# A gated recurrence over rows: the next gates' products move into the branch, and x_par by rows is built from transposes

## The chip, the cores and the metric

The kernel runs on one core of a Trainium2 chip. The metric is the device time of one execution in microseconds (us); the time before is the median of three runs.

## The reference

Four graph layers work on x (16 graphs of 1024 nodes with 256 features, fp32) and a weighted adjacency adj (16 × 1024 × 1024, about 3% non-zero). Each layer normalizes x by rows, applies a ReLU, runs its graph operation and adds the result to x. Only layer 2 matters here. It is a recurrence over the nodes, one after the other:

```
for i in 0..1023:                        # for all 16 graphs
    x_par = row_i(norm_adjT) @ h         # parents' states, updated or not yet
    r, z  = sigmoid(split(x_i @ Wioux.T + x_par @ Wiouh.T + biases))
    hc    = tanh(x_i @ Wcoux.T + (x_par * r) @ Wcouh.T + biases)
    h_i   = z * x_par + (1 - z) * hc
```

A node needs the new states of only those earlier nodes that it has an edge with.

## The kernel before

Layers 0 and 1 run first, one graph at a time, then layer 2 for all graphs, then layer 3, one graph at a time. The change touches layer 2 alone.

Layer 2 walks over 8 blocks (t) of 128 nodes, each cut into 8 sub-blocks (s) of 16 nodes. A sub-block holds 16 nodes of 16 graphs, so 256 rows, kept as two groups g of 128. Inside a sub-block, nodes depend on each other only along short chains of edges. The kernel therefore doesn't go node by node. It repeats a *round* on all 256 rows, each time with the states of the round before, until no chain is longer. Three rounds are always run (K = 3). If the longest chain of a sub-block is longer, a branch runs `one_more`, and inside it a loop runs further rounds. The chain lengths come from the adjacency at the start of the layer (`levels`).

A round works on changes. `change` multiplies the change of the states, dh, by the sub-block's own adjacency `ai` and gets the change of x_par in columns (features on partitions), first in the PSUM tile `px` and then in SBUF as `dx`; it also adds it to `x`, the x_par in columns. `round_` then adds products of dx to three PSUM accumulators that live through the whole sub-block: `pr` for r, `pz` for z, `pc` for the candidate. Four products of 128×128 by 128×256 go to each. ACT and DVE take r, z and hc from them and make the new state. `pxr` is a fourth accumulator: x_par by rows (nodes on partitions), which the new state needs. `seed` starts the accumulators of a sub-block: pr, pz and pc are copied from the gates of the inputs, and pxr gets four transposes of x. Then each `change` adds two products `ai`·dh to pxr.

Other work of TensorE is placed between these steps. There are four kinds.

- *Base products* (`base_tasks`, pb, L360): for the next block, the parents' sum over all other blocks. For each of the 16 graphs 14 matmuls of 128×128 go into one PSUM tile pb, of which there is a single buffer, and DVE moves it to `bxt` (L363). The graph's inputs `ab` and `hb` (1.4 MB together) are loaded through SP's queue into two buffers each, and the load for the graph after the next waits until the present graph's buffer is free. In the first block one more input block is used, in the last block there are no base products.
- *Far products* (`far_tasks`, pf, L461): a finished sub-block's part in the later sub-blocks of its block; up to eight matmuls, moved to bxt by DVE (L464).
- *Near product* (pf, L633): its part in the very next sub-block; x of the next sub-block waits for it.
- *Gates of the next inputs* (`gate_tasks`): x_i times Wx for the next sub-block, two tasks for r (L439, evicted by ACT into `gr`, L441) and two for z and the candidate (L448, evicted by DVE into `gz`, L450). Near, far and gates share the two buffers of pf.

The order in the source: `fill()` is called three times in each of the three rounds, and each call runs some of the base tasks (spread over the block) and some of the queue `others` (far tasks and gates, spread over the sub-block). `one_more` has no fill. At the end of a block, `last_block` (L386) multiplies the states just stored by the last piece of the adjacency, graph by graph, after reading them back from DRAM.

The source order isn't the order on an engine: a scheduler reorders each engine's instructions when the program is built, within the stretches between branches. It doesn't move an instruction across a branch.

## Time and profile before

| what | value |
|---|---|
| median of three runs | 6301.03 us (6299.73 to 6306.5) |
| profiled execution, its own time | 6304.63 us |
| its span | 6302.8 us |
| mean granted TensorE clock | 0.93 |
| TensorE matmul busy | 5568.5 us (88%) |
| TensorE weight load busy | 3827.4 us (61%) |
| VectorE busy | 2503.2 us (40%) |
| ScalarE busy | 1412.6 us (22%) |
| GpSimd busy | 1043.2 us (17%) |
| first x of the recurrence to first product of layer 3 | 1780.6 to 4708.6 us |

The profiled execution is a single one, 3.6 us above the median. Busy shares are means over three stages with different limits; for the recurrence one reads windows of one block or one sub-block. An engine's idle time before an instruction is listed with what ended it: "<-DVE bxt L363" means that VectorE's instruction of line 363 on tile bxt released it, "<-PEq L619" that TensorE's sequencer came through the branch at line 619. In the timeline, x8 means eight records under one line; an fp32 matmul makes two records, an fp32 transpose one.

### The profile page before, as it was taken

The page shows a single profiled execution, that of the slowest core. Times are in us where ns is not written, and L with a number is a line of the kernel's source. Part 1 is how long each engine was busy: PE and PEld are TensorE (multiplying, and loading weights), DVE is VectorE, ACT ScalarE, POOL GpSimd, SP SyncE. Part 2 cuts the span into 40 slices and gives each one's busy share as a digit, 9 for nine tenths or more (in the row PEclk, how much of TensorE's full clock was granted, in tenths as well). Part 3 has the DMA queues.
Part 4 walks back from the last instruction along what each step waited for, and adds up shares of the span by engine and source line. Part 5 has one row for each costly group of instructions (what it writes and reads, how often), then busy time and mean ns, then how long its engine had stood idle before and what let it go on. Part 6 is the DMA issues. An engine that isn't in the chain of part 4 may idle for free. (4 is left out here: it accounts for less than half of the span.)

```text
span 6302.8 us, 63085 instructions
## 1 busy us (share of the span) xinstructions
PE 5568.5 (88%) x23167; PEld 3827.4 (61%) x23167; DVE 2503.2 (40%) x6257; ACT 1412.6 (22%) x3226; POOL 1043.2 (17%) x1429
## 2 busy tenths in 40 slices
PE   7888888888589898998989989898979999999998
PEld 3444444444378786876777778776755555555555
DVE  2333233332135454554554545454543333233332
ACT  1111111111012222222222212222222222222222
POOL 1222122221111111111111111111111111111110
PEclk9988999889799898998999989898989999999999
DMA  3222122220643332323223233321032212121110
GB/s 127 91 76 100 60 100 81 83 103 21 181 152 98 98 95 59 88 84 91 70 67 102 88 99 98 100 72 34 9 111 74 79 62 94 60 80 69 72 60 14
DMA packets 477355, 520.40 MB, mean 83 GB/s; under 512 B 30208, under 2 KB 428800, under 8 KB 474752
## 3 DMA queue, kind: packets, MB, share of 16 engines
q1 hardware_dynamic: 461056, 447.93, 22.0%
q0 software_dynamic: 15872, 67.18, 2.9%
q8 instruction: 219, 3.59, 0.2%
q14 instruction: 208, 1.70, 0.1%
HBM read 431.10 MB, written 83.95 MB: 82 GB/s over the span
## 5 line engine op out<-in xcount | busy, mean ns | idle before, releaser
L360 PE MATMUL pb<-ab,hb 128*128 128x128 f32 x3648 | 530.4, 286 | 59.7 <-DMA hb<-he_d 34.8
L360 PEld LDWEIGHTS pb<-ab,hb 128*128 128x128 f32 x3648 | 511.1, 201 | 101.5 <-issue 43.3
L152 PE MATMUL pa<-at,h 128*128 128x512 f32 x1024 | 478.2, 631 | 72.0 <-ACT h L142 72.0
L686 PE MATMUL pa<-at,h 128*128 128x512 f32 x1024 | 444.5, 595 | 31.4 <-ACT h L83 31.4
L719 PE MATMUL pa<-w,hT 128*128 128x256 f32 x2048 | 468.2, 384 | 0.0
L699 PE MATMUL ph<-w,ag 128*128 128x512 f32 x1024 | 452.7, 593 | 0.0
L152 PE MATMUL pa<-at,q 128*128 128x512 f32 x1024 | 443.7, 594 | 0.0
L157 DVE COPY ag<-pa 128x512 f32<-128x512 f32 x64 | 44.3, 692 | 980.1 <-PE pa L152 980.1
L719 PEld LDWEIGHTS pa<-w,hT 128*128 128x128 f32 x2048 | 385.7, 193 | 46.5
L152 PEld LDWEIGHTS pa<-at,h 128*128 128x128 f32 x1024 | 206.2, 203 | 337.1 <-issue 241.9
L686 PEld LDWEIGHTS pa<-at,h 128*128 128x128 f32 x1024 | 195.8, 191 | 270.9 <-issue 267.6
L520 DVE TENSOR_TENSOR r<-r,x 128x256 f32<-128x256 f32 x450 | 173.3, 427 | 451.4 <-ACT r L519 451.4
L152 PEld LDWEIGHTS pa<-at,q 128*128 128x128 f32 x1024 | 193.6, 190 | 250.3 <-issue 237.7
L519 ACT ACTIVATE r<-pr 128x256 f32<-128x256 f32 x450 | 148.7, 382 | 844.4 <-PE pr L479 844.4
L699 PEld LDWEIGHTS ph<-w,ag 128*128 128x128 f32 x1024 | 191.1, 190 | 214.8 <-issue 214.0
L479 PE MATMUL pc<-wh,drx 128*128 128x256 f32 x1288 | 310.8, 384 | 10.4 <-DVE drx L522 10.4
L479 PE MATMUL pr<-dx,wh 128*128 128x256 f32 x1288 | 314.5, 383 | 0.0
L479 PE MATMUL pz<-wh,dx 128*128 128x256 f32 x1288 | 310.7, 380 | 0.0
L541 DVE TENSOR_TENSOR w<-w,hc 128x256 f32<-128x256 f32 x450 | 188.4, 454 | 266.8 <-ACT hc L540 266.8
L479 PEld LDWEIGHTS pc<-wh,drx 128*128 128x128 f32 x1288 | 237.4, 190 | 79.1 <-DVE drx L522 29.4
L704 ACT ACTIVATE junk<-hh 128x512 f32<-128x512 f32 x256 | 161.2, 630 | 527.3 <-DVE hh L702 527.3
L479 PEld LDWEIGHTS pr<-dx,wh 128*128 128x128 f32 x1288 | 242.2, 193 | 42.7 <-issue 3.3
(168 smaller groups left out, 8478.1 us busy)
## 6 DMA issues: line engine op xcount, KB each, us to landing
at<-in_adjT SPq DMA_DIRECT2D x128, 1024.0 KB
ab<-in_adj SPq DMA_DIRECT2D x128, 512.0 KB
x<-in_x SPq DMA_DIRECT2D x16, 1024.0 KB
x_d<-x POOLq DMA_DIRECT2D x16, 1024.0 KB, 7.5
he_d<-h POOLq DMA_DIRECT2D x16, 1024.0 KB, 5.1
heT_d<-hT POOLq DMA_DIRECT2D x16, 1024.0 KB, 4.5
he<-heT_d SPq DMA_DIRECT2D x16, 1024.0 KB
hb<-he_d SPq DMA_DIRECT2D x16, 1024.0 KB
```

Of the source, the lines that this page charges most:

```text
L152: nc.tensor.matmul(pa, h[:, mt, c * P : (c + 1) * P], at[:, mt, n0 : n0 + 512], start=mt == 0, stop=mt == NT - 1)
L157: nc.vector.tensor_copy(ag[:, c, n0 : n0 + 512], pa)
L360: nc.tensor.matmul(pb[:, c], hb[:, j, c * P : (c + 1) * P], ab[:, j], start=j == jts[0], stop=j == jts[-1])
L479: nc.tensor.matmul(to, lhsT, rhs, start=False, stop=True, skip_group_check=True)
L519: nc.scalar.activation(r[:, e], pr[:, e], AF.Sigmoid)
L520: nc.vector.tensor_mul(r[:, e], r[:, e], x[:, e])
L541: nc.vector.tensor_mul(w[:, g], w[:, g], hc[:, g])
L686: nc.tensor.matmul(pa, h[:, mt, c * P : (c + 1) * P], at[:, mt, n0 : n0 + NH], start=mt == 0, stop=mt == NT - 1)
L699: nc.tensor.matmul(ph, ag[:, c, (t0 + t) * P : (t0 + t + 1) * P], w1[:, c, e * 512 : (e + 1) * 512], start=c == 0, stop=c == DC - 1)
L704: nc.scalar.activation(junk, to, AF.Square, accum_out=sq[:, t, e : e + 1])
L719: nc.tensor.matmul(po, hT[:, k, t * P : (t + 1) * P], w2[:, k], start=k == 0, stop=k == HC - 1)
```

## The change

There are two edits.

1. x_par by rows. `seed` no longer transposes x into pxr, and `change` no longer adds the two products `ai`·dh. In their place `round_` calls `to_rows` after the products into pr: four transposes of dx (of x in the first round), which are accumulated in pxr.
2. Gates. The four gate tasks of the next sub-block no longer go to the queue that `fill` empties. If the branch for further rounds is taken, `one_more` runs them: two before its round and two in its fills. If it isn't taken, an else arm runs all four. Their list is turned round, since `one_more` takes from its end.

```diff
-                return (gr, gz), deque([task_r(0), task_r(1), task_z(0), task_z(1)])
+                return (gr, gz), [task_z(0), task_z(1), task_r(0), task_r(1)]
...
-            def seed(base, gr, gz):
+            def seed(gr, gz):
                 nc.scalar.activation(pr, gr, AF.Copy)
-                for g in range(G2):
-                    for c in range(DC):
-                        nc.tensor.matmul(pxr[:, g, c * P : (c + 1) * P], base[:, c, g * GR : (g + 1) * GR], ident,
-                                         is_transpose=True, start=g == 0 and c == 0, stop=True, skip_group_check=True)
...
             def change(dh, x, ai):
...
-                for g in range(G2):
-                    add(pxr[:, g], aig[g], dh[:, g])
...
+            def to_rows(dx, first):
+                for g in range(G2):
+                    for c in range(DC):
+                        nc.tensor.matmul(pxr[:, g, c * P : (c + 1) * P], dx[:, c, g * GR : (g + 1) * GR], ident,
+                                         is_transpose=True, start=first and g == 0 and c == 0, stop=True,
+                                         skip_group_check=True)
...
             def round_(...):
                 for e in range(DC):
                     for c in range(DC):
                         add(pr[:, e], wh[:, c, e * P : (e + 1) * P], dx[:, c])
+                to_rows(dx, first)
...
-            def one_more(x, rx, h, ho, ai):
+            def one_more(x, rx, h, ho, ai, tasks=()):
+                tasks = list(tasks)
+                def fill():
+                    if tasks:
+                        tasks.pop()()
...
                 dx = change(dh, x, ai)
-                r = round_(dx, x, rx, None, lambda: None, h)
+                fill()
+                fill()
+                r = round_(dx, x, rx, None, fill, h)
...
                     if s + 1 < NS:
                         sub = load_sub(t, s + 1, dp)
                         gx, tasks = gate_tasks(he, s + 1)
-                        others.extend(tasks)
...
-                    with tc.If(n_more[0][s] > 0, preferred_fallthrough_block=False):
-                        one_more(x, rx, h, ho, ai)
+                    with tc.If(n_more[0][s] > 0, preferred_fallthrough_block=False) as more_or_not:
+                        one_more(x, rx, h, ho, ai, tasks)
...
+                    if tasks:
+                        with more_or_not.Else():
+                            for task in tasks:
+                                task()
```

## The prediction

> **What bounds the kernel now.** I read first the busy shares, then the windows of one block of the recurrence (block 4, where no extra round runs), then the groups of instructions with shapes kept apart (window 1780 to 4680), then the timeline. The two stages around the recurrence are untouched by the diff, so only the 2.93 ms from 1781 to 4709 us count.

> Windows of block 4, one per sub-block (columns: width, then busy us and count of PE, PEld, DVE, ACT, POOL, then TensorE clock, DMA share, GB/s):

> ```profile
> 3366.80:3406.60 39.80, 38.66 (x205) 30.89 (x204) 22.39 (x50) 10.13 (x24) 7.05 (x11) 1.00 0.33 105
> 3520.10:3552.90 32.80, 32.23 (x178) 27.09 (x177) 18.00 (x48) 10.13 (x24) 4.51 (x9) 1.00 0.41 122
> ...
> sum 323.00, PE 301.81 PEld 251.51 DVE 159.30 ACT 80.88 POOL 54.73; mean PE 37.73 PEld 31.44 DVE 19.91 ACT 10.11 POOL 6.84
> ```

> TensorE is busy 38.66 of 39.80 us while VectorE has 22.39: TensorE's own work sets the length. Of the block's 21.2 us of TensorE idleness some 12.6 lie in the hand-over to the next block, so the rounds hold about 8.6. They have so little because other products (pb, far, gates) stand in each round's waits. Groups of instructions, then the timeline of the very last sub-block, which has no such filling:

> ```profile
> L360 PE MATMUL pb<-ab,hb 128*128 128x128 f32 x3137 | 458.2, 282 | 8.4 <-DMA hb<-he_d 3.3 <-DVE bxt L387 3.1 <-DVE bxt L363 1.4
> L448 PE MATMUL pf<-wx,hs 128*128 128x512 f32 x496 | 236.3, 595 | 3.4 <-PEq L621 2.0 <-PEq L619 1.4
> L439 PE MATMUL pf<-hs,wx 128*128 128x256 f32 x496 | 126.9, 381 | 0.0
> L479 PE MATMUL pxr<-dh,ai 128*128 128x256 f32 x388 | 104.2, 390 | 0.0
> L633 PE MATMUL pf<-bd,h 128*128 128x128 f32 x448 | 72.6, 311 | 83.5 <-DVEq L621 57.3 <-PEq L619 12.5 <-DVE h L542 7.2
> ```

> ```profile
> 4660.82 1.13 PE L497 MATMUL px<-ai,ho 128*128 128x128 f32 x8 [1.75 <-DVE ho L542]
> 4661.78 1.03 PE L479 MATMUL pxr<-ho,ai 128*128 128x256 f32 x4
> 4662.65 1.89 PE L479 MATMUL pr<-dx,wh 128*128 128x256 f32 x8
> 4664.38 1.89 PE L479 MATMUL pz<-wh,dx 128*128 128x256 f32 x8
> 4666.14 1.99 PE L479 MATMUL pc<-wh,drx 128*128 128x256 f32 x8
> 4669.89 1.13 PE L497 MATMUL px<-ai,dh 128*128 128x128 f32 x8 [1.75 <-DVE dh L542]
> ```

> An fp32 matmul is two records, a transpose one. From starts: px 0.9 us, the pxr adds 0.86, pr, pz, pc 1.73 each; then 1.9 us from pc's end until tanh and the DVE adds let the next px go. Between px's end and pr lie 0.94 us for copying dx, which the pxr adds fill exactly. So a bare round has two holes, **1.92** and **0.94** us.

> [...] pb has one buffer, and where products into it follow each other (last_block) the trace shows the bubble:

> ```profile
> 3305.57 1.22 PE L386 MATMUL pb<-ao,hr 128*128 128x128 f32 x4 [0.51 <-DVE bxt L387]
> ...
> 1745.57 3.81 PE L360 MATMUL pb<-ab,hb 128*128 128x128 f32 x32 [3.34 <-DMA hb<-he_d]
> 1750.55 3.81 PE L360 MATMUL pb<-ab,hb 128*128 128x128 f32 x32 [1.18 <-DMA hb<-he_d]
> ```

> [...] here the 1.4 MB of a batch (ab and hb), issued from 3001.40, moved between 3002.4 and 3007.2:

> ```profile
> 3002.40:3007.20 4.80, 4.77 (x30) 4.35 (x30) 2.69 (x7) 0.38 (x1) 0.29 (x1) 1.00 0.91 296
> ```

> so 5.7 to 6 us from release to data[...]. [...] the block hand-over runs at 0.78, the bare rounds with 1.9 us gaps at 1.00. [...]

> **The change part by part**, with the instruction order of both built programs, which matters more than the diff, since a scheduler places instructions between branches.

> *x_par by rows.* Removed: two pxr adds (0.86 us) in each later round. Added: four transposes of dx between pr and pz; before, those in the first round ran at 0.44 us for four (four records, next start 0.44 to 0.49 later). First round: moved only. Per block 16 × (0.44 − 0.86) = −6.7 us of TensorE work. But the adds sat in the 0.94 hole, and the transposes are on the path (pr, transposes, pz, pc back to back; drx is ready 3.5 us after pr begins, TensorE reaches pc after 3.9). So it pays only where something else fills the hole.

> *Gates.* Eight matmuls per sub-block: 4 at 0.43 and 4 at 0.86 (L439, L448 starts), 5.16 us, with two 0.47 us ACT evictions and two 0.69 us DVE ones. They leave the queue that fill() empties and go to the branch. In the else arm they hide the 1.92 us until h and the wait of near (L633); their evictions hide under near and the x add (1.7 us; gr 0.67 plus the pr copy 0.60 is less). No DMA moves; POOL's hs copy is done earlier.

> *What the scheduler makes of it.* In blocks 0 to 6 the built program issues, right after the branch of sub-blocks 0 to 3 and **ahead of near**, a burst of 24 to 31 pb matmuls; then few pb in the rounds, and none at all from the fourth or fifth sub-block's end on. Before, none stood there: 41, 31, 36, 36, 26, 18, 18, 18 were spread over the rounds. Near is queued behind the burst, and behind near x, pr and the whole round. The burst's work (0.223 us each: the opening phase runs 16 of them from 1675.36 to 1678.93) is not new, but it is now where nothing needs cover, and two things are new.

> (a) Bubbles in the burst. It crosses two batch ends (14 matmuls each): 2 × 0.55 us for pb's one buffer. And the load of batch b+2 may start only when b's buffer is free: 6.0 us later data, while b+1 occupies 3.1 + 1.1, so 1.8 us more. 2.9 us × 4 per block = +11.6. Bounds: 1.1 us each if loads keep up; some 4 if they take the 7 us per batch of the opening phase (from 1738 to 1746).

> (b) Cover gone. Holes left open, walked through the new order: sub-block 0: 0.58+0.27+0.36+0.72=1.9; 1 to 3: 1.3, 1.0, 1.0; 4: 2.3; 5: 5.0; 6: 5.5; 7: 0.8+2×(1.92+0.94)=6.5. Sum 24.5 against 8.6: +16. Bounds: 0.5 to 1.3 times that, since far evictions on DVE may shift the holes.

> Per block −6.7+11.6+16=+21, times 7: **+147**. Block 7 has no pb before or after; it loses the gates as filling: −6.7 against about +15 of holes, **+8**.

> *Taken branch.* 29 of 64 sub-blocks take it (from the inputs' adjacency), 33 extra rounds. Before, an extra round costs near's wait (57.3/22 = 2.6 us) and 1.1 for px beside 6.9 of matmuls. Now gates fill these, and in 13 sub-blocks the burst covers near's wait: −3 × 13; in the other 16, where near still waits for h: −1 each. **−55** (bounds −20 and −80).

> Sum: 147+8−55 = +100 on the profiled execution's 6304.6; its time lies 3.6 above the median of 6301.0, so the median should be **6401**.

> **The rivals.** *Faster:* the gates turn waits into work and TensorE stays full. Then only −6.7×8 and −55 and the else arms' share of near's wait (12.5) remain: 6301−54−55−12 = **6180**. For it: 83.5 us idle before near. Against it: the burst, and bare rounds at the end of each block. It decides below an added idleness of 15 us per block (I count 28). 8%. *Worse:* the loads also slip to 7 us and each burst's stall brings a half-clock window (3.4 us wide in the clock record, half lost): 28 × (1.1+1.7) more, **6480**; for it the 0.78 at hand-overs, against it the 1.00 over 1.9 us gaps. 20%. *Bubbles hidden:* loads keep up and half of (b) holds: −50−57, **6295**, no change; 4%. *Not what it says:* the transposes overwrite instead of adding; then values differ, and the time is that of the forecast. The forecast itself: 68%.

> **Numbers.** A measurement of this kernel can tell 0.2%, 12.6 us. Slower takes the forecast and the worse case, 0.88; same 0.04; faster 0.08. The range, 6325 to 6510, runs from the forecast with bubbles at their low bound and most cover kept to the worse case with (b) at its high bound.

> **What would show it.** After: pb (L360) with idleness before it of some 80 us, by DVE bxt and DMA hb; near's idleness fallen from 83.5 below 40; sub-blocks 0 to 3 of a block longer by 4 to 10 us (gates and pb of others moved in), 5 and 6 hardly shorter though they lost 4 us of pb; PE's busy sum lower by some 60 us while the stage is longer. Wrong if pb's idleness stays under 20 us, or if sub-blocks 5 and 6 fall by over 3 us.

## The result, and the profile after

The changed kernel takes **6492.8 us** (median, 6491.0 to 6500.55) against 6300.4 us before on the same chip: 1.0306 times the time before, 95% interval 1.0288 to 1.0324. The forecast was 6401 with a range from 6325 to 6510. So the sign is right and the time lies in the range, but the loss is 192 us where 100 was worked out.

The profiled execution has a span of 6490.9 us and a mean clock of 0.922. On the page's busy line TensorE is busier than before (5588.9 us against 5568.5), although its products should take some 60 us less:

```profile
PE 5588.9 (86%) x23167; PEld 3824.9 (59%) x23167; DVE 2468.4 (38%) x6257; ACT 1408.7 (22%) x3226; POOL 1019.6 (16%) x1429
```

Windows of block 4 after, one per sub-block (columns as before). Shown are sub-blocks 0, 1 and 5, and the sum:

```profile
3430.90:3479.40 48.50, 45.48 (x265) 39.32 (x266) 17.37 (x43) 10.04 (x24) 4.21 (x8) 0.94 0.52 134
3479.40:3523.10 43.70, 41.39 (x231) 33.80 (x230) 21.10 (x49) 10.05 (x24) 7.66 (x14) 1.00 0.38 121
...
3645.90:3679.40 33.50, 29.74 (x142) 23.78 (x140) 17.68 (x45) 9.98 (x25) 4.44 (x9) 0.95 0.26 76
...
sum 348.40, PE 306.21 PEld 251.69 DVE 155.67 ACT 80.36 POOL 51.82; mean PE 38.28 PEld 31.46 DVE 19.46 ACT 10.04 POOL 6.48
```

Sub-block 1 went from 39.8 to 43.7 us. Sub-block 5 has 36 fewer matmul records (142 against 178) and is no shorter: 33.5 against 32.8. The block's sum rose by 25.4 us. Groups of instructions in the recurrence (window 1780 to 4880, shapes apart):

```profile
L360 PE MATMUL pb<-ab,hb 128*128 128x128 f32 x3200 | 435.4, 287 | 97.3 <-DMA hb<-hn_d 36.1 <-DMA hb<-he_d 27.3 <-DVE bxt L363 18.9
L479 PE MATMUL pr<-dx,wh 128*128 128x256 f32 x1288 | 351.9, 416 | 34.6 <-DVE dx L496 32.9 <-DVE bxt L464 1.7
...
L386 PE MATMUL pb<-ao,hr 128*128 128x128 f32 x448 | 136.4, 460 | 113.9 <-DMA hr<-hn_d 59.2 <-DVE bxt L387 46.6 <-issue 6.7
...
L493 PE MATMUL px<-ai,dh 128*128 128x128 f32 x776 | 118.7, 299 | 128.6 <-DVE dh L545 65.9 <-DVE dh L557 62.6
...
L647 PE MATMUL pf<-bd,h 128*128 128x128 f32 x448 | 65.5, 294 | 17.1 <-DVE h L545 7.8 <-DVEq L631 6.2 <-POOL ai L416 3.1
```

The idle time ahead of the base products went from 8.4 to 97.3 us, two thirds of it ended by a load. Near's fell from 83.5 to 17.1. The holes of the rounds opened: ahead of px for dh 128.6, ahead of pr for dx 34.6. Ahead of last_block's products (L386) 113.9 us stand in place of 96.8. The same three groups before:

```profile
L479 PE MATMUL pr<-dx,wh 128*128 128x256 f32 x1288 | 314.5, 383 | 0.0
...
L386 PE MATMUL pb<-ao,hr 128*128 128x128 f32 x448 | 136.4, 460 | 96.8 <-DVE bxt L387 46.6 <-DMA hr<-hn_d 42.4 <-issue 7.3
...
L497 PE MATMUL px<-ai,dh 128*128 128x128 f32 x776 | 112.4, 287 | 51.7 <-DVE dh L548 36.8 <-DVE dh L542 14.7
```

The timeline at the end of block 4's sub-block 0 shows the burst; gates of the else arm, then base products, and only then near:

```profile
3463.68 3.60 PE L448 MATMUL pf<-wx,hs 128*128 128x512 f32 x8
3467.12 2.08 PE L439 MATMUL pf<-hs,wx 128*128 128x256 f32 x8
3469.04 0.38 PE L360 MATMUL pb<-ab,hb 128*128 128x128 f32 x2
3469.93 3.39 PE L360 MATMUL pb<-ab,hb 128*128 128x128 f32 x28 [0.52 <-DVE bxt L363]
3474.88 3.52 PE L360 MATMUL pb<-ab,hb 128*128 128x128 f32 x28 [1.55 <-DMA hb<-hn_d]
3478.24 1.06 PE L647 MATMUL pf<-bd,h 128*128 128x128 f32 x8
```

**Three shares of the recurrence.** To compare kernels I split its length (first x to first product of layer 3) into TensorE's idle time (neither matmul nor weight load), the clock loss (half of the time that TensorE was busy while the clock was granted at half) and the rest, which stands for the work at full clock. All three are worked out from the trace, in us. The clock loss is an estimate: it assumes that work at half clock lasts twice as long (in before, six records into pr took 2.65 us at half clock and 1.46 at full). A row's shares are those of one profiled execution, which lies up to 12 us from the median.

| kernel | median | ratio to before (95%) | recurrence | idle | clock loss | rest |
|---|---|---|---|---|---|---|
| before | 6300.4 | 1 | 2928.0 | 306.7 | 127.8 | 2493.5 |
| after | 6492.8 | 1.0306 (1.0288 to 1.0324) | 3105.6 | 457.1 | 178.9 | 2469.5 |
| e1 rows only | 6288.8 | 0.9989 (0.9980 to 0.9997) | 2912.4 | 319.0 | 156.7 | 2436.7 |
| e2 gates only | 6513.6 | 1.0354 (1.0340 to 1.0368) | 3118.2 | 445.9 | 137.5 | 2534.8 |
| e3 hold base | 6320.4 | 1.0040 (1.0026 to 1.0053) | 2937.7 | 344.8 | 145.1 | 2447.8 |
| e4 before branch | 6228.6 | 0.9892 (0.9877 to 0.9908) | 2854.8 | 284.8 | 107.7 | 2462.3 |
| e5 three buffers | 6417.8 | 1.0201 (1.0187 to 1.0215) | 3058.3 | 426.9 | 154.9 | 2476.4 |
| e6 one in arms | 6303.5 | 1.0014 (1.0007 to 1.0021) | 2923.4 | 329.0 | 139.3 | 2455.1 |
| e7 straight, old rows | 6217.6 | 0.9882 (0.9867 to 0.9897) | 2836.8 | 248.6 | 67.3 | 2520.9 |
| e8 hand-over only | 6261.8 | 0.9944 (0.9932 to 0.9957) | 2873.4 | 279.7 | 93.2 | 2500.5 |
| e9 hold, hand-over | 6302.9 | 1.0009 (1.0000 to 1.0018) | 2924.7 | 329.9 | 145.8 | 2449.0 |
| e10 best, two tiles | 6167.4 | 0.9792 (0.9778 to 0.9805) | 2786.2 | 239.6 | 42.6 | 2504.0 |
| e11 before, two tiles | 6232.8 | 0.9897 (0.9882 to 0.9912) | 2856.4 | 307.5 | 72.6 | 2476.2 |
| e12 after, two tiles | 6393.8 | 1.0156 (1.0141 to 1.0171) | 3010.3 | 429.2 | 123.7 | 2457.3 |

Each ratio is to the kernel before on the same chip in the same series; its medians there were 6295.6 to 6300.4. From before to after: idle +150, clock loss +51, rest −24, and 10 us that lie ahead of the recurrence. That is the 188 us between the two profiled spans.

### The profile page after: what moved, and what is told of

Same layout as the page of the kernel before. It is cut to its first block, busy times and chain, and to the rows that moved or that the text cites. A ratio compares the mean times of both kernels' runs of the same rounds, so it can differ in the third digit from the quotient of the medians.

```text
span 6490.9 us, 63160 instructions
## 1 busy us (share of the span) xinstructions
PE 5588.9 (86%) x23167; PEld 3824.9 (59%) x23167; DVE 2468.4 (38%) x6257; ACT 1408.7 (22%) x3226; POOL 1019.6 (16%) x1429
## 5 line engine op out<-in xcount | busy, mean ns | idle before, releaser
L360 PE MATMUL pb<-ab,hb 128*128 128x128 f32 x3648 | 501.1, 290 | 156.7 <-DMA hb<-he_d 67.1
L360 PEld LDWEIGHTS pb<-ab,hb 128*128 128x128 f32 x3648 | 477.0, 204 | 195.2 <-issue 110.6
L479 PE MATMUL pr<-dx,wh 128*128 128x256 f32 x1288 | 351.9, 416 | 34.6 <-DVE dx L496 32.9
L479 PE MATMUL pz<-wh,dx 128*128 128x256 f32 x1288 | 311.2, 380 | 0.0
L479 PEld LDWEIGHTS pr<-dx,wh 128*128 128x128 f32 x1288 | 255.0, 208 | 92.8 <-issue 47.3
L479 PE MATMUL pc<-wh,drx 128*128 128x256 f32 x1288 | 305.4, 380 | 0.6
L479 PEld LDWEIGHTS pc<-wh,drx 128*128 128x128 f32 x1288 | 242.6, 190 | 49.4 <-issue 13.9
L728 PE MATMUL pt<-ident,hh 128*128 128x128 f32 x1024 | 193.1, 325 | 83.3 <-DVE hh L724 74.2
```

The source lines that it names most:

```text
L360: nc.tensor.matmul(pb[:, c], hb[:, j, c * P : (c + 1) * P], ab[:, j], start=j == jts[0], stop=j == jts[-1])
L479: nc.tensor.matmul(to, lhsT, rhs, start=False, stop=True, skip_group_check=True)
L728: nc.tensor.transpose(pt[:, t * P : (t + 1) * P], hh[:, t, k * P : (k + 1) * P], ident)
```

## The experiments

Where nothing else is said, a diff is against the changed kernel; it is cut to its core.

**e1: the first edit alone.** The gates go into the queue that fill() empties, as in the kernel before.

```diff
-                return (gr, gz), [task_z(0), task_z(1), task_r(0), task_r(1)]
+                return (gr, gz), deque([task_r(0), task_r(1), task_z(0), task_z(1)])
...
+                        others.extend(tasks)
...
-                        one_more(x, rx, h, ho, ai, tasks)
+                        one_more(x, rx, h, ho, ai)
```

> The first edit alone: x_par by rows from transposes of the change, gates as before in the fill queue. The built program has no burst of base products ahead of near. Theory (the gates' place lets the scheduler put the burst ahead of near and leaves the rounds bare): this run is faster than before, some 6250 us (-161 x 0.42 us of TensorE work, +15 us in the 33 bare extra rounds), base products' idleness stays under 20 us. Rival (the transposes on the path are the cause): slower, 6370 us or more (161 x 0.44 us on the path).

Measured: 0.9989 of before. The rest fell by 57 us (by count, 54 without the extra rounds and 68 with them), but idle rose by 12 and clock loss by 29. In block 7, which has no base products to fill a hole, the edit costs 13 us: idle +6, clock loss +15, rest −8. In its groups the hole that the pxr products used to cover shows as a wait for dx, and near waits as before:

```profile
L479 PE MATMUL pr<-dx,wh 128*128 128x256 f32 x1288 | 336.0, 401 | 24.8 <-DVE dx L496 24.8
...
L636 PE MATMUL pf<-bd,h 128*128 128x128 f32 x448 | 76.5, 323 | 84.6 <-DVEq L624 57.0 <-PEq L622 12.3 <-DVEq L622 8.1
```

So the first edit is not what slows the kernel, and it is worth hardly anything by itself.

**e2: the second edit alone.** Gates in the arms, x_par by rows as before: transposes of x in seed and two pxr products in each change.

```diff
+                for g in range(G2):
+                    add(pxr[:, g], aig[g], dh[:, g])
...
-                to_rows(dx, first)
```

> The second edit alone: gates in both arms of the branch, x_par by rows as before (transposes of x at the start, adds of the adjacency's products in each change). The built program has bursts of 28 to 30 base products ahead of near. Theory: slow like the changed kernel, 6480 to 6560 us, idleness before base products near 90 us. Rival (transposes are the cause): 6300 to 6420 us.

Measured: 1.0354, as the theory expected. The whole loss comes with the gates in the arms. It is 0.0048 more than with both edits, so beside gates in the arms the first edit saves some 30 us. By shares, gates in the arms bring idle +139, clock loss +10 and rest +41; the first edit on top of them (after against e2) brings +11, +41 and −65.

**e3: both edits, but no burst.** The base tasks that fill() issues are ordered behind the last near product, so none can stand ahead of it.

```diff
-                        for _ in range(-(-len(todo) // left)):
-                            todo.popleft()()
+                        with ExitStack() as held:
+                            if todo is base_todo and last_near is not None:
+                                held.enter_context(tc.issue_after(last_near.ins))
+                            for _ in range(-(-len(todo) // left)):
+                                todo.popleft()()
```

> Both edits, and the base products that fill() issues in a sub-block may not be issued before the near product of that sub-block (an ordering on TensorE, no wait). The built program has no burst, and the base products stand in the rounds as before. Theory: the loss is gone and the first edit's gain shows, 6210 to 6280 us; near's idleness below 30 us. Rival (the gates standing in a row at the branch, in arms of their own, cost the time): stays above 6400 us.

Measured: 1.0040, which neither side expected: 168 us less than after (from the ratios), yet 23 us over before in the same series, where the theory had it faster. Its groups show what stays:

```profile
L360 PE MATMUL pb<-ab,hb 128*128 128x128 f32 x3136 | 454.5, 279 | 18.7 <-DVE bxt L363 7.7 <-issue 3.8 <-DVE bxt L387 3.1
...
L493 PE MATMUL px<-ai,dh 128*128 128x128 f32 x776 | 127.0, 309 | 115.1 <-DVE dh L557 70.0 <-DVE dh L545 42.0
...
L651 PE MATMUL pf<-bd,h 128*128 128x128 f32 x448 | 62.0, 282 | 32.3 <-DVEq L635 20.7 <-DVE h L545 7.6 <-POOL ai L416 2.1
```

The burst's 97.3 us are down to 18.7, but px still waits 115.1 us. So that wait doesn't come from the burst; e4 shows that it goes with the gates' place in the arms.

**e4: both edits, the gates in straight code just ahead of the branch, none in the arms.**

```diff
-                    with tc.If(n_more[0][s] > 0, preferred_fallthrough_block=False) as more_or_not:
-                        one_more(x, rx, h, ho, ai, tasks)
+                    for task in tasks:
+                        task()
+                    with tc.If(n_more[0][s] > 0, preferred_fallthrough_block=False):
+                        one_more(x, rx, h, ho, ai)
```

> Both edits, but the four gate tasks stand ahead of the branch in straight code, and neither arm has any. The built program has no burst (one base product ahead of near). Theory: it is the else arm that makes the scheduler place the burst, so this is fast too, 6220 to 6290 us. If gates as filling in the taken arm are worth what the prediction said (55 us), it is some 40 us slower than the run with held base products; if they are worth little, within 15 us of it. Rival (gates out of the fill queue leave the rounds bare, whatever the scheduler does): above 6400 us.

Measured: 0.9892, as expected, faster than both kernels. It is 92 us faster than e3, where the expectation had it slower or alike. Its groups:

```profile
L360 PE MATMUL pb<-ab,hb 128*128 128x128 f32 x3139 | 460.0, 279 | 5.7 <-DVE bxt L387 3.1 <-DVE bxt L363 2.2 <-issue 0.5
...
L493 PE MATMUL px<-ai,dh 128*128 128x128 f32 x776 | 117.5, 293 | 64.2 <-DVE dh L557 41.3 <-DVE dh L545 19.5
L386 PE MATMUL pb<-ao,hr 128*128 128x128 f32 x448 | 113.8, 398 | 82.7 <-DVE bxt L387 39.5 <-DMA hr<-hn_d 30.4 <-POOL ao L382 8.1
...
L645 PE MATMUL pf<-bd,h 128*128 128x128 f32 x448 | 61.7, 282 | 15.4 <-DVEq L633 11.9 <-DVEq L631 3.4
```

Near waits as little as after (15.4), px nearly as little as before (64.2), there is no burst, and the hand-over (L386) waits less than in either. The built order says how, and the trace agrees: gates that the source has ahead of the branch run partly behind it, where near or last_block would wait. This corrects a sentence in the section on the kernel: the scheduler does place instructions on the other side of a branch. In no run here did it take them out of an arm.

**e5: the changed kernel with a third buffer for ab and hb,** the load two graphs ahead, and one buffer each for gr, gz and hs.

```diff
-                    ab = big.tile([P, NT, P], F32, name="ab")
+                    ab = big.tile([P, NT, P], F32, name="ab", bufs=3)
...
-                    hb = big.tile([P, NT, D], F32, name="hb")
+                    hb = big.tile([P, NT, D], F32, name="hb", bufs=3)
...
-                            if b + 1 < B:
-                                load(b + 1)
+                                load(1)
+                            if b + 2 < B:
+                                load(b + 2)
```

> The changed kernel whole, with three buffers each for the inputs ab and hb of the base products instead of two, and the load issued two graphs ahead; gr, gz and hs get one buffer each to make room. The burst of base products after the branch stays (32 to 35 of them). Theory (part of the burst's cost is the wait for a load that may start only when a buffer is free): the idle time of pb that ends with a DMA, 63 us in the recurrence of the changed kernel, goes, and with it some of the half-clock windows; 6400 to 6460 us. Rival (the burst costs because of where it stands and by pb's single PSUM buffer, and a load that comes earlier only lets TensorE reach the next wait earlier): 6480 to 6510 us, with pb's idle time put down to DVE bxt instead.

Measured: 1.0201, within the theory's range. In its timeline three crossings of a graph's end in a burst cost 0.52 us each and no load is waited for; one of them:

```profile
3419.82 0.94 PE L361 MATMUL pb<-ab,hb 128*128 128x128 f32 x6 [0.52 <-DVE bxt L364]
```

Of the gain, 47 us lie in the recurrence (idle −30, clock loss −24, rest +7) and 29 ahead of it, where the opening phase of base products is paced by the same loads (first x at 1762 in place of 1791).

**e6: one gate task of four in the arms,** three ahead of the branch.

```diff
+                    while len(tasks) > 1:
+                        tasks.pop()()
                     with tc.If(n_more[0][s] > 0, preferred_fallthrough_block=False) as more_or_not:
```

> Both edits, but only one of the four gate tasks (half of z and the candidate, two of the eight products) in each arm; the other three stand ahead of the branch. In the built order the burst after the branch is still there in sub-blocks 0 to 4, with 14 to 20 base products instead of 24 to 31. Theory (the loss comes from the burst that the else arm brings and grows with it; the gates in the arms cost their share besides): about half of the burst's 170 us and a quarter of the arms' 92 us on top of 6229, so 6310 to 6370 us. Rival 1 (an else arm costs its whole price whatever stands in it): over 6440 us. Rival 2 (only the number of gates in the arms counts): 6240 to 6260 us.

Measured: 6303.5 us, just under the theory's range and outside both rivals'. With half the burst the base products' idle time is still 86.5 us, ended mostly by pb's eviction, with loads no longer among the first three:

```profile
L360 PE MATMUL pb<-ab,hb 128*128 128x128 f32 x3168 | 443.9, 288 | 86.5 <-DVE bxt L363 49.2 <-issue 11.3 <-ACT pc L485 6.9
```

So the loss grows with what stands in the arms: none, one task, four tasks give 0.9892, 1.0014, 1.0306. The idle time ahead of pb does not grow with it: it is nearly that of after (97.3), in a kernel 184 us faster. What parts the two kernels lies elsewhere, ahead of px (73.7 in place of 157.9 us), of last_block (84.7 in place of 113.9) and of pr for dx (13.7 in place of 34.6). The bubbles in the burst are thus not what parts the two; the cover that the rounds and the hand-over lose, to the burst and to the arms, weighs more.

**e7: e4 without the first edit** (diff against e4).

```diff
+                for g in range(G2):
+                    add(pxr[:, g], aig[g], dh[:, g])
...
-                to_rows(dx, first)
```

> The gates in straight code ahead of the branch, none in the arms, and x_par by rows as in the kernel before (transposes of x in seed, two pxr products in each change), so the faster version without the first edit. Theory (with gates and base products left to fill the holes, the first edit is worth its arithmetic, 6.7 us per block): 6265 to 6290 us. Rival (as by itself in the kernel before, it is worth about a tenth of a per cent, and moving the gates to just ahead of the branch brought the whole gain): 6228 to 6248 us.

Measured: 0.9882 (0.9867 to 0.9897), which can't be told from e4's 0.9892, and lies below both ranges: without the first edit the kernel is not slower. The rest is 59 us larger than in e4, but idle is 36 and clock loss 40 us smaller. In its groups pr doesn't wait (25.6 us in e4), pc waits 15.2 for drx instead, and the hand-over less:

```profile
L479 PE MATMUL pc<-wh,drx 128*128 128x256 f32 x1288 | 313.5, 385 | 15.2 <-DVE drx L522 15.2
...
L386 PE MATMUL pb<-ao,hr 128*128 128x128 f32 x448 | 106.3, 377 | 61.1 <-DVE bxt L387 35.9 <-DMA hr<-hn_d 15.5 <-POOL ao L382 6.4
```

The products that the first edit saves were work in a hole; with them there, the clock loss is smaller (67.3 us against e4's 107.7).

**e8: the kernel before, with the gates of the block's last sub-block alone ahead of the branch** (diff against before).

```diff
                         gx, tasks = gate_tasks(he_next, 0)
-                        others.extend(tasks)
+                        ahead = list(tasks)
...
+                    for task in ahead:
+                        task()
                     with tc.If(n_more[0][s] > 0, preferred_fallthrough_block=False):
```

> The kernel before, with only the gate tasks that a block's last sub-block makes for the next block taken out of the queue and put in straight code just ahead of the branch; all other gates stay in the queue, and x_par by rows is as before. In the built order ten of those sixteen records now stand after the branch and between the first products of last_block. Theory (the gain of the straight versions lies at the seven hand-overs, whose last sub-blocks took 55 us less in all than before, because the gates fill the wait for the states' reload and keep TensorE's clock): 6235 to 6260 us. Rival (the gain lies in the waits of near inside the blocks, and the hand-over only shows work moved there): 6280 to 6305 us.

Measured: 0.9944, 6261.8 us: 2 us above the theory's range, 18 below the rival's. The last sub-blocks of blocks 0 to 6 took 473.6 us in place of 514.9. By the medians that is about half of the gain of e7. In e7 the same sub-blocks took 460.1 us, so the hand-overs hold some 55 of the 91 us by which its recurrence is shorter than that of before; the rest lies elsewhere.

**e9: e3, with the gates of the last sub-block alone ahead of the branch** (diff against e3).

```diff
+                    if s == NS - 1:
+                        for task in tasks:
+                            task()
+                        tasks = []
                     with tc.If(n_more[0][s] > 0, preferred_fallthrough_block=False) as more_or_not:
```

> The version with both edits whose base products are held behind near, and in it the gates of a block's last sub-block alone in straight code ahead of the branch; the other seven sub-blocks keep theirs in the two arms. Theory (of the 92 us between the held version at 6320 and the straight one at 6229, a good part is the hand-over, where gates in arms can't fill the wait of last_block): 6275 to 6300 us. Rival (gates in arms cost inside the blocks, in the rounds that lost them as filling): 6305 to 6325 us.

Measured: 1.0009 against e3's 1.0040, so some 20 us, and between the two ranges. That is not the whole of the hand-over, because two sets of gates can stand there and the edit moves one. In the traces of before and of e4 a block's last sub-block, up to the first x of the next block, runs 16 products of gates and the first sub-block none: those of the first have been taken up into the hand-over too. In e3 and e9, as in after, it is 8 and 8, since the first sub-block's gates stand in its arms.

By place, the recurrence of e9 is 70 us longer than that of e4 (e3: 83). In blocks 0 to 6 the last and the first sub-block give 28 of it (e3: 47), sub-block 6 gives 24 and the other five together −1; block 7 gives 19. Block 7 has no base products, so no burst and nothing that could be held: its 19 us come from gates in the arms alone. Elsewhere no run parts the arms from the hold, which e3 and e9 have and e4 has not, and the 24 us of sub-block 6 stay open.

**e10, e11, e12: two PSUM tiles in last_block.** The profile of before had shown last_block at half clock throughout (0.50 from 3303.8 to 3331.6 us). The edit, put on e7, on before and on after, lets every second graph use a pf tile:

```diff
-                        pb = psum.tile([P, DC, P], F32, name="pb")
+                        if b % 2:
+                            pb = psum.tile([P, DC, P], F32, name="pf", bufs=2)
+                        else:
+                            pb = psum.tile([P, DC, P], F32, name="pb")
```

> The straight version with the old x_par by rows (6218 us), and in last_block every second graph's product goes to a PSUM tile pf in place of pb, so that DVE's move of one graph lies beside the next graph's matmuls. Theory (the 0.5 us that TensorE waits for bxt L387 in each 1.7 us of last_block keeps a slice of 3.41 us at 30% idle, which is too much for the clock to come back, so that the waits and the half clock fall together): last_block's sixteen steps at some 0.55 us in place of 1.73, up to 15 us at each of seven hand-overs, less what its gates gain already: 6110 to 6170 us. Rival (the load of the states or DVE sets last_block's pace, or the clock stays down for another reason): 6195 to 6225 us.

> The kernel before with the same single edit of last_block. Theory: here the half clock of the hand-over lasts 34 us, so 12 to 18 us go at each of seven hand-overs: 6175 to 6215 us. Rival (pace set elsewhere): 6280 to 6300 us.

> The changed kernel with the same single edit of last_block. If the hand-over is a cost that both kernels have alike, the edit takes from this one what it takes from the kernel before, and the two stay about 190 us apart: 6365 to 6410 us. If the changed kernel's loss came in part from a longer half clock at the hand-over, it takes more from this one than from the kernel before by over 20 us.

Measured: e10 0.9792, 6167.4 us, in the theory's range and the fastest kernel here. e11 6232.8 us, a gain, but 18 us short of the theory's range. e12 6393.8 us, in its range, but the edit takes 1.50% of before's time from after and 1.03% from before. That is 30 us more, the second case of the expectation, and the two kernels stay 161 us apart in place of 190. Last_block in the trace of e11, timeline and group:

```profile
3587.89 1.20 PE L389 MATMUL pb<-ao,hr 128*128 128x128 f32 x4 [9.70 <-DMA hr<-hn_d]
3588.88 1.06 PE L389 MATMUL pf<-ao,hr 128*128 128x128 f32 x4
...
3593.56 0.39 PE L389 MATMUL pf<-ao,hr 128*128 128x128 f32 x2
3599.17 1.22 PE L389 MATMUL pb<-ao,hr 128*128 128x128 f32 x4 [5.22 <-POOL ao L382]
```

```profile
L389 PE MATMUL pb<-ao,hr 128*128 128x128 f32 x224 | 53.0, 379 | 101.6 <-DMA hr<-hn_d 71.2 <-POOL ao L382 29.3 <-issue 0.6
```

Eight graphs take 6.1 us where they took 13.9 (8 × 1.73), and then TensorE waits 5.22 us for the next `ao`. The waits for bxt (46.6 us in before) are gone, but waits for ao (29.3) have come, and the wait for the reload of the states grew from 42.4 to 71.2 us; why it grew is not known. This is what e11 fell short by: its idle time is that of before (307.5), and the gain is 55 us of clock loss and 17 of the rest. From after the edit takes the same 55 us of clock loss, and 28 of idle besides, since there the wait for the reload was long already (59.2 us ahead of L386) and didn't grow (59.3 in e12). So what the edit takes more from after is a wait; the half clock at the hand-over costs both kernels alike.

## Why the prediction was right, and where its size was off

**Right, with sizes.**

- *The burst and its bubbles (a).* Forecast 11.6 us a block, 81 in all; the idle time ahead of pb rose by 89. A crossing shows 0.52 for pb's one buffer and 1.55 for the load, where 0.55 and 1.8 were worked out. e3 shows that the burst, with the cover that it takes from the rounds, is a cause (168 us), and e5 that the loads are (47 us in the recurrence). A second buffer for pb in the burst was not tried, and e6 shows that these bubbles by themselves don't set the loss.
- *Cover gone (b).* Forecast 16 a block and 15 in block 7, together 127. Measured: px<-dh +77, px<-ho +8 (29.3 against 21.4), pr<-dx +35, pr<-x +12.5, together +132, of which 26 lie inside the branch (below) and 106 here. (pc's wait for drx fell by 10, so 96 with it.)
- *Near and the sub-blocks.* Near was foretold below 40 and measured 17.1. Sub-blocks 5 and 6 were to be hardly shorter: in block 4 they took 33.5 and 32.0 us, from 32.8 and 34.7. The second, 2.7 shorter, is close to the 3 us that would have spoken against the forecast. Sub-blocks 1 to 3 grew by 3.9, 4.9 and 6.4, as foretold (4 to 10); sub-block 0 by 13.3, more than that.
- *The first edit.* −6.7 a block where something else fills the hole: e1's block 4 took 315.5 us in place of 323.0.

The forecast's own sum was −54 of work and +153 of idle time (81 + 127 − 55). Idle rose by 150. (For matmuls alone, over all groups within the recurrence, it rose by 156: pb 86, px and pr 132, last_block 17 up; near and far 64, pc, gates and pxr 15 down. Weight loads fill the difference.) That the idle sum held is luck: errors of both signs met, as the next list shows.

**Wrong in size.**

- *Taken branch, −55.* Of this −51 fall to the 29 extra rounds of blocks 0 to 6. What these blocks take over block 4 was 344 us before and 322 after: **−22**. This reckoning hangs on one block (for e9, whose arms are those of e3 up to the last sub-block, it gives 282 against 321), so a second one compares sub-blocks at the same place of a block, with and without the branch taken. The 13 with a burst came out 31 us shorter (forecast 39), the other 12 came out 5 us longer (forecast 12 shorter), each by its scatter to within some 10 us. So the part that the burst takes over came out nearly as forecast, and the second part failed. The step had the gates fill px's wait of 1.1 us a round in the branch as well. But there px waits for dh of one_more, and gates and base products at the end of the stretch ahead had covered part of that wait: it (L548 before, L557 after) went from 36.8 to 62.6 us. The hand-over's +17 was not in the forecast either; against both stands (b), which came out at least 21 lower than forecast.
- *The clock, 0.* The objection to the rival "worse" was that bare rounds with 1.9 us holes run at 1.00. That failed after the change. Counting the half-clock stretches of the recurrence by the product with the longest wait in the 3.41 us before (the length of the shortest of these stretches): behind px 34 after, 8 before (clock loss 59.8 against 13.3 us); behind base products 14 against 1 (24.0 against 1.7); behind near 3 against 15 (7.9 against 28.1); at the hand-overs and the recurrence's end 87.1 against 84.7. Sum **+51**. So the rival had the right second mechanism, but named the burst as its place, where the bare rounds weigh twice as much (+46.5 against +22.3). That its price of 1.7 for each of 28 bursts comes near to 51 in all is chance. By edit, most of it goes with the first: +29 in e1, +41 from e2 to after and +40 from e7 to e4, against +10 in e2. This fits the counts of the last section: the products that it takes out of the 0.94 us hole had kept the idle time of a slice down (pr waits 24.8 us for dx in e1, and not at all in before). The rival's other half, loads at 7 us, did not come: the crossing above costs 2.1 us (0.52 and 1.55), where such loads meant some 4.
- *Block 7, +8.* Measured **+22.3**: idle +10.6 where +15 was forecast, rest −2.2 where −6.7 was, and clock loss +13.9, which the forecast left out.
- *Work, −54.* Measured −24. e1 has −57; e2 alone shows +41 and e7 +27 in the rest, so moving the gates added work time there. It isn't so with every move: e3 and e9, whose gates left the queue too, have −46 and −44. Where these 30 us come from stays open.
- *Ahead of the recurrence, 0.* The first x comes 10 us later (1791 against 1781). Before, 48 base products ran among the second sub-block's gates at the opening; after, 260 stand in one line, paced by loads. e5 supports the loads as the pace; the order by itself wasn't tried.
- *A sign that failed.* TensorE's busy sum was to fall by some 60 us and rose by 20. The forecast had no new half-clock slices, and in them products last longer: in before, six records into pr took 2.65 us at half clock (from 4652.96) and 1.46 at full (from 4642.69).
- *The rivals that fell.* Nothing of "faster" or "bubbles hidden": pb's idle time is 97 us. The time can't decide on "not what it says", which has the time of the forecast. That the transposes add and don't overwrite was the author's assumption; no trace here shows values.

From 100 to 188: taken branch and other idle time −3 together, work +30, clock +51, opening +10.

What the arms cost beside the burst was foreseen only in part, as holes in the rounds: e3 has no burst and is 92 us slower than e4. In these runs gates in an arm filled only that arm. Gates in straight code ran in e4 on both sides of the branch and between the products of last_block, for two sub-blocks at once.

## What to carry to other kernels

Work put into the arms of a run-time branch was lost here as filling for all that lies around it, and it changed where the scheduler put the rest; give such work to straight code ahead of the branch first, and read the built order of both. Count a hole together with its neighbours before calling it harmless: in these profiles each of the 360 slices of 3.41 us at full clock in which the matmuls idled for over 2.1 us was followed by one at half clock. Where the clock is at half for long stretches, look for small periodic waits, here 0.51 us in each 1.73 for the one PSUM tile pb. Don't price a wait by its own sum alone: pb's idle time was nearly the same in two kernels 184 us apart. And products that were saved in a hole were not time saved here: e1's rest fell by 57 us, its time by 0.11%.

## What the hardware showed that was not expected

```profile
3375.72:3379.13 3.41, 3.41 (x17) 2.88 (x16) 1.91 (x5) 1.20 (x4) 0.00 (x0) 1.00 0.00 0
3379.13:3382.55 3.42, 0.97 (x8) 0.74 (x7) 2.12 (x5) 0.58 (x2) 0.61 (x1) 1.00 0.00 0
3382.55:3385.96 3.41, 3.41 (x12) 2.87 (x11) 1.18 (x3) 0.86 (x3) 0.00 (x0) 0.50 0.02 5
3385.96:3389.37 3.41, 3.41 (x19) 2.95 (x19) 0.66 (x2) 1.09 (x3) 0.00 (x0) 1.00 0.00 0
```

A slice with 0.97 us of matmuls is followed by one at 0.50; after one full slice the clock is back. Counted from 1781 to 4600 us in all fourteen profiles, by the idle time of matmuls in a slice:

| slice runs at | idle in it, us | next slice full | next slice half |
|---|---|---|---|
| full | under 1.3 | 9398 | 0 |
| full | 1.3 to 2.1 | 411 | 140 |
| full | over 2.1 | 0 | 360 |
| half | under 0.3 | 429 | 0 |
| half | 0.3 to 0.7 | 70 | 63 |
| half | over 0.7 | 0 | 678 |

So no full slice with under 1.3 us of idle time was followed by one at half clock, and every one with over 2.1 us was; between them both happened (411 and 140). A half slice was always followed by a full one where it idled for under 0.3 us, and never where it idled for over 0.7. This fits that a bare round, with holes of 1.9 and 0.9 us, sometimes brings a half-clock slice and sometimes not (behind px, 34 stretches after and 8 before); that it goes by where the grid cuts the round is an estimate from these counts. It also fits that the hand-overs of before stayed at half clock for 34.13 us (six) and 37.55 us (one). There last_block's waits of 0.51 us in each 1.73 leave a slice idle for 1.0 us. At full clock no slice with that little was followed by a half one (0 of 9398), and at half clock none with that much by a full one (0 of 678):

```profile
3313.92:3317.34 3.42, 2.44 (x8) 1.85 (x8) 0.79 (x3) 0.00 (x0) 1.26 (x1) 0.50 0.07 21
```

Two tiles in place of one took 55 us of clock loss away in e11 and in e12, if not all of it: the stretch of e11 shown above, from 3587.9 to 3605.0, still ran at 0.77.
